# Attention and a mixture of experts in one kernel: queries and keys turned through DRAM, projections in pairs, inverse roots by log and exp

## The chip, the cores and the metric

The kernel runs on one core of a Trainium2 chip. The metric is the device time of one execution in microseconds (us), lower is better. The engines have a name each in the profile: PE is TensorE (matmuls; PEld its weight loads), DVE is VectorE, ACT is ScalarE, POOL is GpSimd, SP is SyncE, which here only issues DMAs.

## What is computed

The input x has 16 batches of 512 rows of 128 numbers, all in 32-bit floats. After a layer norm, two branches read the same normalised rows, and both are added to x:

```python
def _l2norm(t):
    n = jnp.sqrt(jnp.sum(t * t, axis=-1, keepdims=True))
    return t / jnp.maximum(n, EPS)
...
q, k, v = (proj(Wq), proj(Wk), proj(Wv))      # 16 heads of 8 numbers
q = _l2norm(q)
k = _l2norm(k)
sim = jnp.einsum('bhid,bhjd->bhij', q, k) * SCALE
sim = jnp.where(causal, mask_value, sim)
attn = jax.nn.softmax(sim, axis=-1)
o = jnp.einsum('bhij,bhjd->bhid', attn, v)
...
logits = jnp.einsum('bsh,eh->bse', x, Wr)     # 8 experts, the best 2 of each row
probs = jax.nn.softmax(logits, axis=-1)
top_v, top_i = jax.lax.top_k(probs, K)
for e in range(E):
    h = jax.nn.gelu(jnp.einsum('bsh,mh->bsm', x, W1[e]) + b1[e], approximate=False)
    y = jnp.einsum('bsm,hm->bsh', h, W2[e]) + b2[e]
    out = out + y * w_e[..., None]
...
x = x + attention(xn) + experts(xn)
```

## The kernel before

The kernel has three parts in time. First come the attention of batches 0 to 13 with the routing of all rows to experts beside it, then 71 expert blocks of 256 rows each, and last the attention of batches 14 and 15, beside which the experts' results are fetched and added.

A batch's attention is ten stages (`PER = 10`; `PAIR = 5` stages for two of the four groups of heads). Stage t of the whole program issues, in this order: the scores of stage t (`scores`, L665, into two of three PSUM buffers of the pool `ps_sim`, each of two banks) and their two exponentials on ScalarE (L675); one side step on TensorE in the first 21 stages (turning normalised rows, router logits); the causal masks of the stage before, on VectorE (L686) or GpSimd; the weighted sums of the stage two before (`LAG = 2`; `weigh`, L708, all into the one PSUM tile `av`), and after the last sums of a head group, in stages 1, 4, 6 and 9 of a batch, the transpose of `av` into `mid` on VectorE (L720); and then whatever `plan` holds for that stage (`due`). TensorE, VectorE, ScalarE and SyncE run their instructions in exactly the order in which these calls are written, so the numbers given to `at_stage` decide who stands behind whom. GpSimd keeps an order of its own through `on_pool` (L502), where the 128 indirect DMAs that send rows to the experts' slots are interleaved with squares and masks.

`prep(b)` puts the preparation of a batch into `plan`, at stages counted from its own first stage `t0`:

```python
times = (-18, -17, -14, -11) if b > 1 else (-11, -11, -10, -9)
...
    (-7, lambda: values(2)), (-7, sums), (-7, root_start), (-7, root_step),
    (-6, root_step), (-5, root_step), (-4, scale), (-3, turn_q), (-2, turn_k),
    (-2, lambda: alone(0)), (-1, lambda: alone(1)), (0, lambda: alone(2)),
    (b != B - 1, lambda: alone(3)),
```

`proj` projects 128 rows to q, k and v at once (L561) into the single PSUM buffer `misc`, which transposes, router logits and the output projection also use, and ScalarE copies the result to `qkv` (L564). GpSimd squares q and k (`squares`) and copies v into `vaug` (`values`). `sums` adds the squares by head on VectorE (L585), `root_start` takes the maximum with a tiny number (L600) and guesses the inverse root by integer arithmetic, and three calls of `root_step` refine it with three small VectorE instructions each (L211 to L213). `scale` (L608) multiplies. `turn_q` and `turn_k` turn the rows by four TensorE transposes each into `misc` (L619, L626) and copy the result on VectorE (L621, L628). `alone(r)` (L634) makes the keys' quarter r of `kT`, in which all but one head in four is zero. The first batch is prepared at the start of the program, with Sqrt on ScalarE and a reciprocal. `finish(b)` divides by the softmax's sums, turns the result and applies the output projection (`wout`, L752).

An expert block loads its rows and both weights (`fetch`, six buffers, five blocks ahead), turns the rows (L796), and does two matmuls (L817, L828) with a Gelu between (L820).

Of the kernel before, what the change touches and what calls it, by code (L numbers as in the profile page):

```python
# [10 lines left out]
F32 = mybir.dt.float32  # L11
# [6 lines left out]
HEADS = 16  # L18
# [6 lines left out]
def attention_moe_kernel(  # L25
# [45 lines left out]
    FIRST = B - 2  # L71
    AHEAD = (FIRST - 1) // 2
# [101 lines left out]
    def SIM(name):  # L174
# [4 lines left out]
        p1.tile([P, NC, HEADS, VW], F32, tag=f"vaug{n}", name=f"vaug{n}") for n in range(2)  # L179
# [34 lines left out]

    def guess(y, var):

        nc.vector.tensor_scalar(
            y.bitcast(I32), var.bitcast(I32), -0.5, float(0x5F3759DF), ALU.mult, ALU.add
        )
        nc.vector.tensor_single_scalar(var, var, -0.5, ALU.mult)  # L220

    def scales(b0, b1, root):
# [7 lines left out]
        def variance():  # L230
# [9 lines left out]
            if root:  # L240
                nc.scalar.activation(var, var, AF.Sqrt)

        def first():
            guess(rstd[:, cols], have["var"])
            newton(rstd[:, cols], have["var"], have["dif"], 1)

        def second():
            newton(rstd[:, cols], have["var"], have["dif"], 2)

        def shifts():  # L250
            if root:
                nc.vector.reciprocal(rstd[:, cols], have["var"])
            dif = have["dif"]
            nc.vector.tensor_add(dif, even, odd)
            nc.vector.scalar_tensor_tensor(
                shift[:, cols], dif, -0.5, rstd[:, cols], ALU.mult, ALU.mult
            )

        return [variance, shifts] if root else [variance, first, second, shifts]
# [14 lines left out]
    def turn_x(b, bank, copy):  # L274
# [3 lines left out]
        copy(xnT[b], bank)  # L278

# [271 lines left out]
    def prep(b):  # L551
# [3 lines left out]
        s["vaug"] = vaugs[b % 2]  # L555

        def proj(c, bank=misc):
            if not c:
                s["qkv"] = p2.tile([P, NC, NQKV], F32, tag="qkv", name=f"qkv{b}")
            pp = bank(f"proj{b}_{c}")  # L560
            nc.tensor.matmul(  # L561
                pp[:, :NQKV], xnT[b][:, ts(c, P)], wall, start=True, stop=True
            )
            nc.scalar.copy(s["qkv"][:, c], pp[:, :NQKV])  # L564

        heads = lambda t: t.rearrange("p c (h d) -> p c h d", d=DH)

# [5 lines left out]

        def values(c):
            on_pool(
                nc.gpsimd.tensor_copy,
                s["vaug"][:, c : c + 2, :, 0:DH],
                heads(s["qkv"][:, c : c + 2, 2 * D : 3 * D]),
            )
# [9 lines left out]
        def root_now(meanwhile):  # L589
# [3 lines left out]
            nc.scalar.activation(s["ss"], s["ss"], AF.Sqrt)  # L593
            meanwhile()
            nc.vector.reciprocal(s["rn"], s["ss"])

        def root_start():

            s["rn"] = sm.tile([P, n], F32, tag="rn", name=f"rn{b}", bufs=1)
            nc.vector.tensor_scalar_max(s["ss"], s["ss"], L2_EPS * L2_EPS)  # L600
            guess(s["rn"], s["ss"])

        def root_step():
            t = sm.tile([P, n], F32, tag="t", name=f"t{b}")
            newton(s["rn"], s["ss"], t, 1)

        def scale():
            nc.vector.tensor_mul(  # L608
                heads(s["qkn"]),
                heads(s["qkv"][:, :, : 2 * D]),  # L610
                s["rn"].rearrange("p (c h) -> p c h", c=NC).unsqueeze(3).to_broadcast(
                    [P, NC, 2 * HEADS, DH]
                ),
            )

        def turn_q():
            pt = misc(f"qt{b}")
            for c in range(NC):
                nc.tensor.transpose(pt[:, ts(c, P)], s["qkn"][:, c, :D], ident)  # L619
            s["qT"] = p2.tile([P, S], F32, tag="qT", name=f"qT{b}")  # L620
            nc.vector.tensor_copy(s["qT"], pt)  # L621

        def turn_k(bank=misc):
            pt = bank(f"kt{b}")
            for c in range(NC):
                nc.tensor.transpose(pt[:, ts(c, P)], s["qkn"][:, c, D:], ident)  # L626
            s["kr"] = p1.tile([P, S], F32, tag="turned", name=f"kr{b}")
# [532 lines left out]
```

## Time and profile before

| what | value |
|---|---|
| median of 3 runs | 779.11 us (777.05 to 779.11) |
| time of the profiled execution | 773.95 us |
| its span, first to last instruction | 772.2 us, mean granted TensorE clock 0.986 |
| start, up to the first scores | 0 to 27.3 us |
| attention of batches 0 to 13, with routing | 27.3 to 430.7 us |
| expert blocks | 430.7 to 707.0 us |
| attention of batches 14 and 15 | 707.0 to 772.2 us |

A row of the timeline gives start and duration in us, engine, line of the kernel, operation, output and inputs, shapes, how many instructions are merged in it, and in brackets how long the engine was idle before and what released it. TensorE's durations overlap a little, as its matmuls are pipelined; the distance from one start to the next is what an instruction costs there.

### The profile page before, as it was taken

What the parts mean: (1) busy time and instruction counts of PE and PEld (TensorE: products, weight loads), DVE (VectorE), ACT (ScalarE), POOL (GpSimd) and SP (SyncE); (2) the same over time, 40 slices, a digit from 0 to 9 for tenths busy, and PEclk for the clock granted to TensorE, in tenths of its full rate; (3) what the DMA queues carried; (4) which work ended last, traced back from release to release, by engine and by line L of the source; (5) the groups of instructions that cost most, each with busy time, mean ns of one, the idle gap of its engine ahead of it and who ended that gap; (6) DMA issues with size and microseconds to landing.
All of it is one profiled execution on the core that took longest, in us unless ns stands there. A gap on an engine that the chain in (4) does not pass through costs nothing.

```text
span 772.2 us, 17655 instructions
## 1 busy us (share of the span) xinstructions
PE 731.1 (95%) x6478; PEld 450.4 (58%) x6478; DVE 516.6 (67%) x1128; ACT 464.8 (60%) x703; POOL 485.9 (63%) x576
## 2 busy tenths in 40 slices
PE   6899999989999999999999899999999999998994
PEld 2344444334334444444444499989999999996441
DVE  6876678798987887887788445455554445442584
ACT  3767676567777778777878544433444444446771
POOL 4658444388898888888888255554555455556441
PEclk9999999999999999999999999999999999999996
DMA  9940000001101111110110698877777787850596
GB/s 264 326 149 2 1 2 1 1 20 32 33 29 37 37 34 33 36 37 29 38 37 32 194 280 229 229 223 210 235 222 226 222 233 224 233 167 6 187 283 183
DMA packets 91829, 96.48 MB, mean 125 GB/s; under 512 B 10956, under 2 KB 69455, under 8 KB 91744
## 3 DMA queue, kind: packets, MB, share of 16 engines
q1 hardware_dynamic: 82240, 78.01, 35.4%
q0 software_dynamic: 8640, 17.06, 6.5%
q8 instruction: 52, 0.85, 0.4%
q10 hardware_dynamic: 864, 0.28, 0.2%
q14 instruction: 33, 0.27, 0.1%
HBM read 64.34 MB, written 31.88 MB: 125 GB/s over the span
## 4 chain that ended last, share of the span: by engine, by line
PE 80%; DVE 14%; DMA 2%; ACT 1%; issue 1%; POOL 1%; DVEq 0%; POOLq 0%
PE sim L665 17%; PE av L708 17%; PE av L828 16%; PE ph L817 16%; PE proj L561 5%; DMA yt<-results 2%; DVE x L908 2%; PE xgt L796 2%; PE po L752 2%; DVE mid L720 1%; PE qt L619 1%; PE kt L626 1%; DVE st L206 1%; PE idle L959 1%; DVE kT L634 1%
## 5 line engine op out<-in xcount | busy, mean ns | idle before, releaser
L675 ACT ACTIVATE ex<-sim 128x1024 f32<-128x1024 f32 x320 | 310.0, 1022 | 105.4 <-PE sim L665 100.7
L502 POOL DMA_INDIRECT results<-y,to x142 | 139.0, 979 | 138.5 <-DVE y L836 111.8
L820 ACT ACTIVATE gT<-ph,bias 128x256 f32<-128x256 f32 x284 | 111.4, 475 | 158.4 <-PE ph L817 154.0
L665 PE MATMUL sim<-qT,kT 32*128 32x512 f32 (+3 forms) x2048 | 190.1, 463 | 0.7 <-ACT ex L675 0.7
L708 PE MATMUL av<-ex,vaug 128*12 128x512 f32 (+3 forms) x2048 | 171.5, 442 | 16.1 <-DVE mid L720 10.0
L502 POOL TENSOR_SCALAR_AFFINE_SELECT ex<-ex 128x512 f32<-128x512 f32 (+1 forms) x144 | 115.2, 808 | 84.3 <-ACT ex L675 82.6
L502 POOL DMA_INDIRECT slots<-rows,pos x128 | 140.7, 1099 | 28.8 <-issue 25.8
L665 PEld LDWEIGHTS sim<-qT,kT 32*128 32x128 f32 x2048 | 95.7, 185 | 77.8 <-issue 34.0
L828 PE MATMUL av<-xnT,gT 128*128 128x128 f32 x1136 | 138.7, 275 | 1.4 <-ACT gT L820 0.9
L817 PE MATMUL ph<-xgT,xnT 128*128 128x256 f32 x568 | 134.7, 380 | 1.5 <-DVE xgT L798 1.5
L828 PEld LDWEIGHTS av<-xnT,gT 128*128 128x128 f32 x1136 | 132.4, 192 | 2.6 <-issue 1.5
L708 PEld LDWEIGHTS av<-ex,vaug 128*12 128x12 f32 x2048 | 43.0, 92 | 129.3 <-issue 85.5
L817 PEld LDWEIGHTS ph<-xgT,xnT 128*128 128x128 f32 x568 | 102.5, 190 | 13.4 <-DVE xgT L798 1.9
L798 DVE COPY xgT<-xgt 128x256 f32<-128x256 f32 x71 | 30.1, 424 | 68.9 <-PE xgt L796 68.7
L833 DVE TENSOR_TENSOR y<-av,bb 128x256 f32<-128x256 f32 x71 | 30.1, 425 | 67.2 <-PE av L828 67.2
L720 DVE STREAM_TRANSPOSE mid<-av 128x512 f32<-128x512 f32 x64 | 45.5, 711 | 40.6 <-PE av L708 40.4
L561 PE MATMUL proj<-wall,xnT 128*128 128x384 f32 x128 | 58.3, 542 | 5.4 <-DVE xnT L278 2.9
L502 POOL TENSOR_TENSOR qkn<-qkv 128x256 f32<-128x256 f32 x64 | 54.9, 867 | 9.9 <-ACT qkv L564 9.5
L686 DVE TENSOR_TENSOR ex<-ex,causal 128x1024 f32<-128x1024 f32 x40 | 52.0, 1300 | 3.4 <-ACT ex L675 3.4
L634 DVE TENSOR_SCALAR kT<-kr,hmask 128x512 f32<-128x512 f32 x64 | 40.5, 635 | 0.6
L564 ACT COPY qkv<-proj 128x384 f32<-128x384 f32 x64 | 30.9, 482 | 14.1 <-PE proj L561 13.9
L561 PEld LDWEIGHTS proj<-wall,xnT 128*128 128x128 f32 x128 | 19.5, 190 | 32.6 <-issue 16.3
(144 smaller groups left out, 584.8 us busy)
## 6 DMA issues: line engine op xcount, KB each, us to landing
xnT<-in_w1T_dram SPq DMA_DIRECT2D x71, 256.0 KB, 3.5
xnT<-in_w2T_dram SPq DMA_DIRECT2D x71, 256.0 KB
slots<-fill SPq DMA_DIRECT2D x48, 198.0 KB, 5.1
xg<-slots SPq DMA_DIRECT2D x71, 132.0 KB
yt<-results SPq DMA_DIRECT2D x16, 512.0 KB, 5.1
bb<-in_b_dram SPq DMA_DIRECT2D x71, 64.0 KB
x<-in_x_dram SPq DMA_DIRECT2D x16, 256.0 KB, 4.7
out_dram<-x SPq DMA_DIRECT2D x16, 256.0 KB, 5.5
```

The lines of the kernel that those rows point to most:

```text
L502: ins = op(*args, **kw)
L561: nc.tensor.matmul(pp[:, :NQKV], xnT[b][:, ts(c, P)], wall, start=True, stop=True)
L564: nc.scalar.copy(s["qkv"][:, c], pp[:, :NQKV])
L634: nc.vector.tensor_scalar_mul(s["kT"][:, r], s["kr"], hmask[:, r : r + 1])
L665: nc.tensor.matmul(halves[g // 2][:, g % 2, col : col + (NC - j) * P], s["kT"][group, r, ts(j, P)], s["qT"][group, j * P :], start=True, s ...
L675: nc.scalar.activation(ex[:, 2 * h : 2 * h + 2], half, AF.Exp, scale=SCALE)
L686: nc.vector.tensor_mul(diag, diag, causal.unsqueeze(1).unsqueeze(1).to_broadcast([P, NG, many, P]),)
L708: nc.tensor.matmul(av[32 * g : 32 * g + VW, j * P :], s["vaug"][:, j, NG * g + r], s[m][:, g, col : col + (NC - j) * P], start=(j == 0), s ...
L720: nc.vector.transpose(s["mid"][:, r], av)
L817: nc.tensor.matmul(ph[:, m], s["w1"][:, ts(m, P)], s["xgT"], start=True, stop=True)
L820: nc.scalar.activation(s["gT"][:, m], ph[:, m], AF.Gelu, bias=bias1[:, i, m : m + 1])
L828: nc.tensor.matmul(py[:, c], s["gT"][:, m, ts(c, P)], s["w2"][:, m], start=(m == 0), stop=(m == NM - 1),)
```

## The change

For batches 3 and later, q and k no longer go through TensorE to change axes. `scale` writes the scaled rows ordered by blocks of 32 numbers, `carry` sends them to a DRAM buffer in four DMAs, each of which takes a quarter of the rows apart into runs of 128 numbers (512 bytes), and a fifth DMA brings them back with the 32-blocks where they belong. What is then left to do is a transpose of 32x32 blocks on VectorE, for q two stages and for k one stage ahead of the batch. All DMAs are issued by SyncE.

Two projections share one of the scores' PSUM buffers, with one copy of q and k for both and one of v, both on ScalarE, v directly into one of three `vaug` tiles. There is one `qkv` buffer in place of two, without v in it.

The inverse roots of the layer norm and of q and k are exp(-ln(v)/2) on ScalarE with one refining step on VectorE, except in the last batch, where the guess and three steps remain. One table with both functions is loaded at the start. Several steps get other stages: the sums and the root come earlier, the first `alone` later in the batches that are carried, and the finishing of a batch one or two stages later. Some of the routing steps move too.

```diff
+    CARRIED = 3
...
-        p1.tile([P, NC, HEADS, VW], F32, tag=f"vaug{n}", name=f"vaug{n}") for n in range(2)
+        p1.tile([P, NC, HEADS, VW], F32, tag=f"vaug{n}", name=f"vaug{n}") for n in range(3)
...
+    def inverse_root(y, var):
+
+        nc.scalar.activation(y, var, AF.Ln)
+        nc.scalar.activation(y, y, AF.Exp, scale=-0.5)
+
+    def refine(y, var, t, steps=1):
+        nc.vector.tensor_single_scalar(var, var, -0.5, ALU.mult)
+        newton(y, var, t, steps)
...
-            if root:
-                nc.scalar.activation(var, var, AF.Sqrt)
...
+            inverse_root(rstd[:, cols], var)
...
+    NF = D // TB
+
+    def berth(name):
+        return dram.tile([NF, TB, 2 * S], F32, tag="berth", name=name, bufs=2)
...
-        def proj(c, bank=misc):
+        def proj(c):
+
             if not c:
-                s["qkv"] = p2.tile([P, NC, NQKV], F32, tag="qkv", name=f"qkv{b}")
-            pp = bank(f"proj{b}_{c}")
-            nc.tensor.matmul(
-                pp[:, :NQKV], xnT[b][:, ts(c, P)], wall, start=True, stop=True
-            )
-            nc.scalar.copy(s["qkv"][:, c], pp[:, :NQKV])
+                s["qkv"] = p1.tile([P, NC, 2 * D], F32, tag="qkv", name=f"qkv{b}")
+            pp = s["pp"] = ps_sim.tile([P, 2, S], F32, tag="sim", name=f"proj{b}_{c}")
+            for k in range(2):
+                nc.tensor.matmul(
+                    pp[:, k, :NQKV], xnT[b][:, ts(c + k, P)], wall, start=True, stop=True
+                )
+                if not b:
+                    nc.scalar.copy(s["qkv"][:, c + k], pp[:, k, : 2 * D])
+            if b:
+                nc.scalar.copy(s["qkv"][:, c : c + 2], pp[:, :, : 2 * D])
+            return lambda: nc.scalar.copy(
+                s["vaug"][:, c : c + 2, :, 0:DH], heads(pp[:, :, 2 * D : NQKV])
+            )
...
+            (inverse_root if b < B - 1 else guess)(s["rn"], s["ss"])
...
+            refine(s["rn"], s["ss"], t, 1 if b < B - 1 else 3)
...
+            if b >= CARRIED:
+                to = s["qkn"].rearrange("p c w -> p (c w)").rearrange(
+                    "p (k c h d) -> p c k h d", c=NC, k=2 * NF, d=DH
+                )
...
+        def carry():
+
+            out_there = berth(f"bqk{b}")
+            to = out_there.rearrange("f i (k t w) -> t i k f w", k=2, t=P // TB)
+            by_block = s["qkn"].rearrange("p c w -> p (c w)").rearrange(
+                "p (k f w) -> p k f w", k=2, f=NF
+            )
+            for t in range(P // TB):
+                nc.sync.dma_start(to[t], by_block[ts(t, TB)])
+            s["z"] = p1.tile([P, 2, S], F32, tag="z", name=f"z{b}")
+            nc.sync.dma_start(
+                s["z"].rearrange("p k s -> p (k s)"),
+                out_there.rearrange("f i n -> (f i) n"),
+            )
+
+        def landed(k):
+            return s["z"][:, k].rearrange("p (t c w) -> p c t w", t=P // TB, c=NC)
...
         def turn_q():
+            s["qT"] = p2.tile([P, S], F32, tag="qT", name=f"qT{b}")
+            if "z" in s:
+                nc.vector.transpose(s["qT"], landed(0))
+                return
...
         def turn_k(bank=misc):
+            s["kr"] = p1.tile([P, S], F32, tag="turned", name=f"kr{b}")
+            if "z" in s:
+                nc.vector.transpose(s["kr"], landed(1))
+                return
...
-        times = (-18, -17, -14, -11) if b > 1 else (-11, -11, -10, -9)
...
-            (-11, lambda: squares(0)), (-11, lambda: squares(1)),
-            (-10 + (b == 1), lambda: squares(2)), (-9 + (b == 1), lambda: squares(3)),
-            (-8, lambda: values(0)),
-            (-7, lambda: values(2)), (-7, sums), (-7, root_start), (-7, root_step),
-            (-6, root_step), (-5, root_step), (-4, scale), (-3, turn_q), (-2, turn_k),
-            (-2, lambda: alone(0)), (-1, lambda: alone(1)), (0, lambda: alone(2)),
-            (b != B - 1, lambda: alone(3)),
...
+        if b >= CARRIED:
+            twos, squared = ((0, -14), (2, -12)), (-13, -13, -11, -10)
+            steps = [
+                (-9, sums), (-9, root), (-7, root_step), (-7, scale), (-7, carry),
+                (-2, turn_q), (-1, turn_k), (-1, lambda: alone(0)),
+            ]
+        else:
+            twos = ((0, -14), (2, -12)) if b > 1 else ((0, -11), (2, -10))
+            squared = (-13, -13, -11, -10) if b > 1 else (-11, -11, -9, -9)
+            steps = [
+                (-7, sums), (-7, root), (-5, root_step), (-4, scale), (-3, turn_q),
+                (-2, turn_k), (-2, lambda: alone(0)),
+            ]
+        for c, t in twos:
+            at_stage(t0 + t, lambda c=c: proj(c)())
+        for c, t in enumerate(squared):
+            at_stage(t0 + t, lambda c=c: squares(c))
+        steps += [(-1, lambda: alone(1)), (0, lambda: alone(2))]
+        for t, step in steps + [(b != B - 1, lambda: alone(3))]:
             at_stage(t0 + t, step)
...
-            at_stage(t0 - 1, lambda: product(0, NG))
-        for n, step in ((0, turn), (2, wout)):
-            at_stage(t0 + n, step)
+            at_stage(t0, lambda: product(0, NG))
+            for n, step in ((2, turn), (3, wout)):
+                at_stage(t0 + n, step)
...
+    nc.scalar.add_instruction(
+        mybir.InstLoadActFuncSet(name=nc.get_next_instruction_name(), act_func_set_id=6)
+    )
```

## The prediction

> **What bounds the kernel now.** I read the page's busy shares and slices first, then the chain that ended last, then one batch of the timeline engine by engine.
>
> ```profile
> PE 731.1 (95%) x6478; PEld 450.4 (58%) x6478; DVE 516.6 (67%) x1128; ACT 464.8 (60%) x703; POOL 485.9 (63%) x576
> PE   6899999989999999999999899999999999998994
> ...
> PE 80%; DVE 14%; DMA 2%; ACT 1%; issue 1%; POOL 1%; DVEq 0%; POOLq 0%
> ```
>
> TensorE is busy in every slice but the first and the last few, and the chain is 80% TensorE. So a TensorE instruction that goes away is worth its full time, and a new wait of TensorE costs its full time. From 234.0 us to 430 us the timeline repeats every 26.49 us (one batch, ten stages) with no TensorE gap over 0.3 us. Two places of that period carry this prediction. The first is the seam between two batches, TensorE's rows and then VectorE's:
>
> ```profile
> 322.52 0.66 PE L626 MATMUL kt<-ident,qkn 128*128 128x128 f32 x4
> 323.10 1.15 PE L665 MATMUL sim<-qT,kT 32*128 32x384 f32 x16
> 324.18 0.62 PE L708 MATMUL av<-ex,vaug 128*12 128x256 f32 x8
> 324.73 0.91 PE L561 MATMUL proj<-wall,xnT 128*128 128x384 f32 x2
> 325.57 1.14 PE L665 MATMUL sim<-qT,kT 32*128 32x512 f32 x8
> ```
> ```profile
> 323.21 0.69 DVE L628 COPY kr<-kt 128x512 f32<-128x512 f32 x1 [1.95 <-PE kt L626]
> 323.94 0.63 DVE L634 TENSOR_SCALAR kT<-kr,hmask 128x512 f32<-128x512 f32 x1
> 324.87 0.72 DVE L720 STREAM_TRANSPOSE mid<-av 128x512 f32<-128x512 f32 x1 [0.31 <-PE av L708]
> 325.51 0.45 DVE L634 TENSOR_SCALAR kT<-kr,hmask 128x512 f32<-128x512 f32 x1
> ```
>
> The new batch's first scores (325.57) read kT, whose first quarter was ready at 324.57, a microsecond early, because the keys were turned a stage before. The second place is two stages later (ScalarE, TensorE, VectorE):
>
> ```profile
> 302.81 3.94 ACT L675 ACTIVATE ex<-sim 128x1024 f32<-128x1024 f32 x4 [0.61 <-PE sim L665]
> ```
> ```profile
> 303.63 1.39 PE L665 MATMUL sim<-qT,kT 32*128 32x256 f32 x16
> 305.00 1.05 PE L708 MATMUL av<-ex,vaug 128*12 128x512 f32 x8
> ```
> ```profile
> 303.77 0.72 DVE L720 STREAM_TRANSPOSE mid<-av 128x512 f32<-128x512 f32 x1 [1.63 <-PE av L708]
> 304.41 0.83 DVE L634 TENSOR_SCALAR kT<-kr,hmask 128x512 f32<-128x512 f32 x1
> ...
> 308.10 1.18 DVE L585 TENSOR_REDUCE ss<-qkn 128x128 f32<-128x1024 f32 x1
> 309.31 0.86 DVE L600 TENSOR_SCALAR ss<-ss 128x128 f32<-128x128 f32 x1
> ```
>
> ScalarE does four exponentials without a pause here, right behind TensorE. TensorE has three score buffers and takes two per stage, so an exponential that is late by more than about a microsecond stops the next scores but one. Last, what a ScalarE instruction that waits for VectorE does to those behind it, from the start of the run:
>
> ```profile
> 19.50 0.40 DVE L592 TENSOR_SCALAR ss<-ss 128x128 f32<-128x128 f32 x1
> 19.93 0.31 ACT L593 ACTIVATE ss<-ss 128x128 f32<-128x128 f32 x1 [1.45 <-DVE ss L592]
> 20.14 0.57 ACT L278 COPY xnT<-xnt 128x512 f32<-128x512 f32 x1
> ```
>
> The copy's matmuls were over at 18.86; it ran only after the root, which waited 1.45 us for VectorE.
>
> **The change, part by part.**
>
> *Transposes of q and k removed* (batches 3 to 15). From 322.52 to 323.10 four of them take 0.58 us of TensorE, eight take 1.16: 13 x 1.16 = **-15.1 us**, all on the path. The two PSUM copies on VectorE (0.69 each) become two block transposes; the nearest row is `mid`, 0.72, so VectorE is as busy as before.
>
> *The trip through DRAM.* Each batch writes 512 KB as 1,024 runs of 512 bytes in four DMAs and reads 512 KB back in rows of 4 KB. The page gives 82,240 packets on SP's queue for 35.4% of 16 engines x 772 us: 53 ns each. 64 runs per engine come to 3.4 us; the row `yt`, also 512 KB, lands in 5.1. With SP's 0.33 to 0.45 us per issue: 1.6 + 3.5 + 0.4 + 5.1 = 10.6 us, estimated. The Trainium skill speaks against such a trip: "VectorE: DVE Perf Modes", The three transpose paths, calls a plain DMA that transposes by its access pattern 19 times slower than the hardware's DMA transpose, for which its table gives 1309 ns per 128x128 block of two bytes. By estimate that is 25 us for a block and 200 for a batch's eight, and the kernel would take over 2 ms. But the rule's condition is a large innermost stride; here innermost runs are contiguous and the 32x32 turning is VectorE's, so I take the row. What is there to hide it: let T be the end of stage 1's weighted sums (303.63 above). VectorE has the maximum done near T + 3.6 (wait B below), then a mask 1.2, reciprocal and product 1.2 to 1.7, four refining steps 1.1 to 2.4 and the scaling 1.2: rows ready near T + 9.3. It asks for q at the end of stage 8, after 17.2 us of TensorE's own rows and 3.0 of wait B, at T + 20.2; 2.7 us more would still cost nothing, as VectorE next waits for TensorE anyway. So zero, with some 3 us of cover. If that is gone, each further microsecond stops VectorE, and TensorE at the seam, 11 times. SP holds nothing else then; with batch 15 the weight fetches stand behind it, five blocks of 3.73 us ahead of their use: zero.
>
> *Wait A, at the seam.* In the changed program batches 3 to 13 turn the keys and mask the first quarter in the last stage before their own scores, behind `mid`, which waits for that stage's weighted sums; the projection that stood on TensorE there is gone. From the end of those sums: 0.14 until `mid` starts, 0.64 to the next instruction, 0.73 for the keys' transpose up to its reader (323.21 to 323.94), 0.63 for the mask, 0.1 to release: 2.24 us with TensorE idle, 1.9 to 2.5 by the shorter and longer rows of L634. I take 2.2: 11 x 2.2 = **+24.2**.
>
> *Wait B, the logarithm.* Root by Ln and Exp puts two ScalarE instructions behind stage 1's exponentials and ahead of stage 2's; Ln waits for VectorE. From T: 0.14 + 0.64 for `mid`, 0.75 for the last mask, 1.21 for the sums, 0.79 for the maximum (L600: mean 747 ns, extremes 0.23 and 1.5), so Ln starts at T + 3.6; the nearest row for it and for Exp is L593, 0.31 each, so the next exponential starts near 4.3 and its buffer is free at 5.4. TensorE wants it after scores (1.08), sums (0.98) and half of the next scores (0.54), at 2.6. Wait: 2.8, from 1.7 to 3.5 by the extremes of L600 and L634. In batches 3 to 14: 12 x 2.8 = **+33.6**, and 0.2 each for ScalarE catching up, **+2.4**. The two waits add, since T moves with A.
>
> *Early roots.* Batches 1 and 2 and the last twelve batches' scales also wait on ScalarE for a loaded VectorE, and in stages 6 and 16 the copy of a new batch waits for the scaling of the last, as there is one qkv buffer now. No row shows it; by the 1.45 above about 1 us each, **+5** (0 to 9). VectorE's own saving, seven small instructions or some 2.7 us a batch, lies beside TensorE: nothing. For batch 15 three refinements and the scaling stand in one place among the expert blocks, 4.3 us against 3.1 before, when a block took 2.4 us longer: **+1.3**.
>
> *Projections in pairs, in the scores' buffers.* Same TensorE work; values now copied by ScalarE (estimated 0.4 twice, for POOL's 0.47 twice), beside longer stages: nothing. Gone are TensorE's waits for the single misc bank (0.79, 0.79, 0.34, 0.56, 0.23, 0.72, 0.38, 0.58, 0.79 up to 151 us): **-5.2**; 1.06 before the first expert block: **-1.1**.
>
> *Waits that shrink as TensorE is later:* 0.29 at stage 2's scores, 11 times, **-3.2**; POOL's (2.20, 0.88, 0.60, 0.89, 0.57 from 166 to 231 us), most: **-4.0**.
>
> *Tables.* Sqrt goes, and with it the second table load, at 24.06 us. The row is 1.28 us with Exp right behind; "ScalarE: Activation LUTs", What ACT_TABLE_LOAD costs, counts 2.66 with its drain. Either way TensorE was held by projections in the misc bank there: **-0.5**, between nothing and 1.3.
>
> Sum: +66.5 - 29.1 = **+37.4**. Against the profiled execution of 774.0 that is 811.4; the median of the runs shown is 779.1, 5 us above it, and I put the sum on that: **816.5 us**.
>
> **Rivals.**
>
> 1. *Faster.* VectorE reaches the first mask and the maximum before TensorE needs them. Without A, B, their follow-up and half of the early waits: 66.5 - 60.2 - 2.5 = 3.8, less 29.1, 754 us. It decides where A and B together fall under some 2.0 us a batch instead of 5.0. For it: VectorE is 67% busy and the order of steps could spare one. Against: both waits start from TensorE's own last sums, which VectorE cannot have earlier. 0.11, with another 0.03 for within 0.3% (what a measurement of this kernel can tell from no change).
> 2. *The trip is late.* At 20 us instead of 10.6, VectorE's wait exceeds its cover by some 6: 11 x 6 = 66, 882 us. Against: DMA busy share 0.11 between 162 and 431 us. 0.05.
> 3. *Ln and Exp don't share a table,* two loads of 1.28 a batch: +33, 850 us. Against: three table loads stand in the changed program, four before. 0.01.
>
> The likeliest, A and B as worked out, has 0.80. Its ends: A 21 to 27, B 20 to 42, follow-up 0 to 7, early 0 to 9, removed waits half to all; not all at one end together, 786 to 838. I keep that as the range: it leaves out most of the faster case and the late trip.
>
> **What would show it.** A batch of near 30 us in place of 26.5; TensorE idle before first scores for VectorE's kT, about 2.2 us; ScalarE idle some 2.5 us before Ln, and TensorE waiting for an exponential one stage later. No `qt`, `kt` in batches 3 to 15, z in SBUF before VectorE asks. I am wrong if batches come out under 26.5 us, or if VectorE waits for a DMA at qT.

## The result, and the profile after

The changed kernel takes 835.93 us in the median of four runs (831.47 to 839.77), the kernel before 779.11 beside it: ratio 1.073, 95% interval 1.068 to 1.079, slower. The profiled execution took 831.47 us (span 829.7, mean granted TensorE clock 0.965; before 0.986), 57.5 us more span than before. The page has for TensorE's busy time, its slices, the granted clock and the chain that ended last:

```profile
PE 756.4 (91%) x6374; PEld 458.7 (55%) x6374; DVE 473.4 (57%) x1036; ACT 469.5 (57%) x737; POOL 459.8 (55%) x544
...
PE   6899999898979988988988979999999999999994
...
PEclk9999997999999999999989999999999999999996
...
PE 79%; DVE 12%; ACT 3%; issue 2%; DMA 1%; POOL 1%; ACTq 0%; POOLq 0%
```

TensorE has 104 instructions fewer and is busy 25 us longer, and its slices have nine eights and two sevens, where they had four eights before. The starts of rows place the 57.5 us (us; an output projection, `po`, ends each batch's work):

| from, to | before | after | more |
|---|---|---|---|
| start, first output projection | 77.4 | 82.2 | 4.8 |
| to the fourth | 97.3 | 98.9 | 1.6 |
| to the thirteenth (nine batches) | 242.6 | 290.9 | 48.3 |
| to the first expert block | 15.4 | 12.1 | -3.3 |
| first to last expert block | 265.5 | 272.4 | 6.9 |
| to the end | 74.1 | 73.2 | -0.9 |

Five of the nine batches take 30.8 to 31.0 us in place of 26.49, the other four 33.7 to 35.0. The seam between two batches, TensorE's rows and then VectorE's:

```profile
321.75 1.15 PE L700 MATMUL sim<-qT,kT 32*128 32x384 f32 x16
322.82 0.62 PE L743 MATMUL av<-ex,vaug 128*12 128x256 f32 x8
325.49 1.14 PE L700 MATMUL sim<-qT,kT 32*128 32x512 f32 x8 [2.04 <-DVE kT L662]
```
```profile
323.51 0.72 DVE L755 STREAM_TRANSPOSE mid<-av 128x512 f32<-128x512 f32 x1 [5.97 <-PE av L743]
324.15 0.67 DVE L651 STREAM_TRANSPOSE kr<-z 128x512 f32<-128x512 f32 x1
324.86 1.24 DVE L662 TENSOR_SCALAR kT<-kr,hmask 128x512 f32<-128x512 f32 x2
```

The first scores of the batch (325.49) now stand still for 2.04 us: `mid`, the keys' transpose and the first mask follow each other on VectorE behind TensorE's own last sums. Two stages later, ScalarE and then TensorE:

```profile
333.36 0.31 ACT L218 ACTIVATE rn<-ss 128x128 f32<-128x128 f32 x1 [2.21 <-DVE ss L600]
333.70 0.31 ACT L219 ACTIVATE rn<-rn 128x128 f32<-128x128 f32 x1
333.92 3.75 ACT L710 ACTIVATE ex<-sim 128x1024 f32<-128x1024 f32 x4
```
```profile
332.62 1.13 PE L700 MATMUL sim<-qT,kT 32*128 32x512 f32 x4
334.98 1.13 PE L700 MATMUL sim<-qT,kT 32*128 32x512 f32 x4 [1.23 <-ACT ex L710]
336.03 1.05 PE L743 MATMUL av<-ex,vaug 128*12 128x384 f32 x16
337.02 1.15 PE L700 MATMUL sim<-qT,kT 32*128 32x384 f32 x16
338.10 0.62 PE L743 MATMUL av<-ex,vaug 128*12 128x256 f32 x8
338.65 2.14 PE L700 MATMUL sim<-qT,kT 32*128 32x512 f32 x8
340.72 0.62 PE L743 MATMUL av<-ex,vaug 128*12 128x512 f32 x4
```

Ln waits 2.21 us for VectorE's maximum with the next exponentials behind it, and the scores that need their buffer take from 332.62 to 336.03, 3.41 us in place of 1.07. The bracket says 1.23 only. Two stages on (338.65 to 340.72) scores take 2.07 in place of 1.07, with no bracket at all. The single matmuls in these rows show why: before, four scores start together (at 312.44, and the next four at 312.97); here they start two at a time (338.65, 339.18, 339.66, 340.20), the four of one buffer first and then the four of the other, whose weight load waits for a semaphore. So TensorE is at work all the time, but on half as many scores at once, and distances between starts are the safer reading. The view of waits, over the whole span (total us, times, longest), TensorE and then ScalarE (before, the first of these waits did not occur and the second was 0.7 us in all):

```profile
PE sim L700 <- DVE kT L662: 22.6, 11, 3.0
PE sim L700 <- ACT ex L710: 16.5, 13, 2.9
```
```profile
ACT rn L218 <- DVE ss L600: 26.9, 14, 2.5
```

The trip through DRAM is not seen in the time: for the batch that begins at 325.49 its first DMA is issued at 308.09, its last packet lands at 316.40, and VectorE turns q at 316.84 without waiting. It is just in time, though; over the 13 batches VectorE waits twice for it, 0.6 us in all.

**The clock.** The trace has stretches of 3.41 us, or a multiple of it, in which the granted TensorE clock is half; they are called half-clock windows here. Below the trace is read in windows of 3.41 us laid on the instants at which the granted clock changes, with TensorE's busy time and count first and PEclk third from the end:

```profile
191.02:194.44 3.42, 2.83 (x28) 1.22 (x26) 0.35 (x1) 2.61 (x5) 3.00 (x3) 1.00 0.12 40
194.44:197.85 3.41, 1.68 (x16) 0.61 (x20) 3.38 (x5) 1.33 (x2) 3.21 (x5) 0.98 0.12 42
197.85:201.26 3.41, 3.41 (x32) 1.31 (x20) 0.88 (x2) 1.43 (x2) 2.93 (x4) 0.52 0.06 20
...
259.29:262.70 3.41, 2.56 (x27) 1.04 (x25) 0.79 (x2) 2.41 (x5) 3.06 (x5) 1.00 0.12 40
262.70:266.12 3.42, 2.23 (x24) 0.69 (x24) 3.30 (x5) 1.69 (x3) 2.93 (x4) 1.00 0.12 40
266.12:269.53 3.41, 3.41 (x56) 2.04 (x48) 0.37 (x1) 2.79 (x3) 2.74 (x4) 1.00 0.13 40
```

At 194.0 to 196.2 the seam's gap falls almost whole into one window (1.73 us of it), and the next window runs at half clock. At 262 the same gap is cut by a window's edge (0.85 and 1.18 us), and the clock stays. Before the last stretch of the span there are thirteen such half-clock windows in the changed kernel, and every one follows a window in which TensorE was idle for 1.1 us or more, or another half-clock window. The kernel before has two.

### The profile page after: what moved, and what is told of

Its sections match the earlier page's. It is cut to its first block, busy times and chain, and to the rows that moved or that the text cites. A ratio compares the mean times of both kernels' runs of the same rounds, so it can differ in the third digit from the quotient of the medians.

```text
span 829.7 us, 17476 instructions
## 1 busy us (share of the span) xinstructions
PE 756.4 (91%) x6374; PEld 458.7 (55%) x6374; DVE 473.4 (57%) x1036; ACT 469.5 (57%) x737; POOL 459.8 (55%) x544
## 4 chain that ended last, share of the span: by engine, by line
PE 79%; DVE 12%; ACT 3%; issue 2%; DMA 1%; POOL 1%; ACTq 0%; POOLq 0%
PE sim L700 20%; PE av L743 18%; PE av L865 15%; PE ph L854 15%; PE proj L572 5%; DVE x L945 2%; DVE mid L755 2%; PE po L787 2%; PE xgt L833 2%; DVE ss L593 2%; ACT ex L710 2%; DVE kT L662 2%; DMA yt<-results 1%; DVE st L207 1%; PE xnt L277 1%
## 5 line engine op out<-in xcount | busy, mean ns | idle before, releaser
L700 PE MATMUL sim<-qT,kT 32*128 32x512 f32 (+3 forms) x2048 | 226.8, 475 | 41.2 <-DVE kT L662 22.6
L700 PEld LDWEIGHTS sim<-qT,kT 32*128 32x128 f32 x2048 | 109.1, 191 | 153.3 <-ACT ex L710 81.3
L509 POOL TENSOR_SCALAR_AFFINE_SELECT ex<-ex 128x512 f32<-128x512 f32 (+1 forms) x142 | 118.3, 841 | 130.5 <-ACT ex L710 122.2
L743 PE MATMUL av<-ex,vaug 128*12 128x512 f32 (+3 forms) x2048 | 179.1, 459 | 8.7 <-DVE mid L755 6.6
L509 POOL DMA_INDIRECT slots<-rows,pos x128 | 135.0, 1055 | 28.0 <-issue 23.9
L854 PE MATMUL ph<-xgT,xnT 128*128 128x256 f32 x568 | 137.8, 386 | 5.9 <-issue 3.5
L509 POOL TENSOR_TENSOR qkn<-qkv 128x256 f32<-128x256 f32 x64 | 44.0, 697 | 42.3 <-issue 20.6
L572 PE MATMUL proj<-wall,xnT 128*128 128x384 f32 x128 | 49.7, 510 | 1.6 <-ACT qkv L576 0.9
L662 DVE TENSOR_SCALAR kT<-kr,hmask 128x512 f32<-128x512 f32 x64 | 36.9, 596 | 0.6
L873 DVE TENSOR_TENSOR y<-y,gate 128x256 f32<-128x256 f32 x71 | 30.2, 425 | 2.4
```

The lines of the kernel that those rows point to most:

```text
L509: ins = op(*args, **kw)
L572: nc.tensor.matmul(pp[:, k, :NQKV], xnT[b][:, ts(c + k, P)], wall, start=True, stop=True)
L662: nc.vector.tensor_scalar_mul(s["kT"][:, r], s["kr"], hmask[:, r : r + 1])
L700: nc.tensor.matmul(halves[g // 2][:, g % 2, col : col + (NC - j) * P], s["kT"][group, r, ts(j, P)], s["qT"][group, j * P :], start=True, s ...
L743: nc.tensor.matmul(av[32 * g : 32 * g + VW, j * P :], s["vaug"][:, j, NG * g + r], s[m][:, g, col : col + (NC - j) * P], start=(j == 0), s ...
L854: nc.tensor.matmul(ph[:, m], s["w1"][:, ts(m, P)], s["xgT"], start=True, stop=True)
```

## The experiments

Ratios are to the kernel before, timed beside each; five rounds each. A batch's length is the distance of output projections in the trace.

**1. The keys one stage earlier** (wait A alone).

```diff
-                (-2, turn_q), (-1, turn_k), (-1, lambda: alone(0)),
+                (-2, turn_q), (-2, turn_k), (-2, lambda: alone(0)),
```

> Only the keys' block transpose and the first mask (and so kT0) move from the last stage before their own scores to the stage before that; everything else is the changed kernel (835.9 us). Theory: wait A is real and additive: the 22.6 us that TensorE waits for kT in the trace go, and the half-clock windows that follow those waits go with them (each costs TensorE about 1.7 us of work, some 3 to 5 of them are at seams): 805 to 815 us, 1.03 to 1.05 of the kernel before, and no row of TensorE scores waiting for VectorE's kT above 0.3 us. Rival: VectorE is as late a stage earlier, because the turned data has not landed from DRAM or because VectorE is behind: then the wait only changes its name, within 8 us of 835.9.

813.03 us, ratio 1.038 (1.036 to 1.040), as the theory had it. The wait for kT falls from 22.6 to 0.3 us. In the execution with the trace (816.41 us, the slowest of five) the clock hardly changes (0.968 for 0.965): wait B is left, and half-clock windows still follow it, at 264, 295, 326 and 357 us. In the other four the clock is 0.976 to 0.980, above all four of the changed kernel (0.959 to 0.968), so clock is part of this gain too.

**2. Ln and Exp one stage later** (wait B alone).

```diff
-                (-9, sums), (-9, root), (-7, root_step), (-7, scale), (-7, carry),
+                (-9, sums), (-9, root), (-8, rooted), (-7, root_step), (-7, scale), (-7, carry),
```

(`root` keeps the maximum, `rooted` is the call of `inverse_root`.)

> Only Ln and Exp of the carried batches' roots move one stage later on ScalarE (behind stage 2's exponentials in place of ahead of them); sums and maximum stay where they are. Theory: wait B is the in-order ScalarE queue behind Ln: 12 x about 2.3 us of TensorE and some 1 us each of ScalarE catching up go, with the half-clock windows behind them: 785 to 805 us, 1.01 to 1.035 of the kernel before. Rival: the root only has a new place to hold up the exponentials, or VectorE, whose refinement follows a stage later, now waits for ScalarE and passes the wait on: within 10 us of 835.9.

816.52 us, ratio 1.042 (1.039 to 1.044): faster than the changed kernel, but less than expected. The waits for exponentials fall from 16.5 to 4.0 us and the clock rises to 0.978, while the weighted sums' wait for `mid` rises from 6.6 to 15.7 us, and an undisturbed batch is 30.0 us in place of 30.8. The wait for kT stays (24.1). So much of what wait B had cost came back as another wait, and a good part of the gain is clock: six half-clock windows before the last stretch in place of thirteen.

**3. Both moves.**

> Both moves together. Theory (A, B and the half-clock windows are the whole loss): granted clock back to 0.98 to 0.99, a batch back under 26.5 us, TensorE 15 us shorter than before by the transposes: 750 to 768 us, 0.96 to 0.985 of the kernel before. Rival 1: the trip through DRAM, no longer covered by wait B (some 3 us), is late: VectorE waits for z, up to 3 us a batch, 770 to 800 us. Rival 2: most of the loss is not in A and B but in the early roots and the DMA traffic: above 790 us.

805.88 us, ratio 1.030 (1.028 to 1.033): the second rival's time, but the rows below show another cause than the one it named. The clock is nearly back (0.983 in the trace, 0.974 to 0.983 in all five), the batch is 29.58 us. The two moves are worth 0.035 and 0.031 alone, taken from 1.073, and 0.043 together. The next batch's rows show what stands in their place, TensorE and then VectorE:

```profile
312.73 1.39 PE L704 MATMUL sim<-qT,kT 32*128 32x256 f32 x16
315.01 1.05 PE L747 MATMUL av<-ex,vaug 128*12 128x512 f32 x8 [0.89 <-POOL ex L509]
315.99 1.14 PE L704 MATMUL sim<-qT,kT 32*128 32x512 f32 x8
319.06 1.05 PE L747 MATMUL av<-ex,vaug 128*12 128x384 f32 x16 [1.93 <-DVE ex L725]
```
```profile
315.15 1.21 DVE L593 TENSOR_REDUCE ss<-qkn 128x128 f32<-128x1024 f32 x1
316.39 1.48 DVE L600 TENSOR_SCALAR ss<-ss 128x128 f32<-128x128 f32 x1
317.80 1.21 DVE L725 TENSOR_TENSOR ex<-ex,causal 128x1024 f32<-128x1024 f32 x1
```
```profile
316.68 1.11 POOL L509 TENSOR_SCALAR_AFFINE_SELECT ex<-ex 128x1024 f32<-128x1024 f32 x1
```

Sums and maximum, which the change put into stage 1, stand ahead of the mask of stage 1's exponentials (317.80), which the weighted sums at 319.06 want 1.93 us earlier. In the changed kernel wait B had covered that. The maximum (316.39) also takes 1.48 us here, and took 0.23 in the changed kernel (333.10 above): a mask of GpSimd runs beside it (last row). That is so in eight batches of this kernel, and in all the traces of this case this maximum takes over 0.7 us only where a GpSimd mask runs beside it for 0.7 us or more. So by the rows 1.25 of the 1.93 us go with what GpSimd does at that moment, and not with the order alone; no run separates the two. The trip, no longer covered by B, is nearly late (SyncE, then VectorE):

```profile
322.92 2.54 SPq L632 DMA_DIRECT2D bqk<-qkn  x4
328.42 0.33 SPq L634 DMA_DIRECT2D z<-bqk  x1
```
```profile
332.12 0.71 DVE L645 STREAM_TRANSPOSE qT<-z 128x512 f32<-128x512 f32 x1 [1.33 <-DMA z<-bqk]
```

It takes 9.2 us from its first issue (322.92) to VectorE's start; VectorE waits 6.3 us for it in all (1.5 at most), and TensorE waits 0.3 us for the keys. The first rival, as the cause of what is left, is out.

**4. Waits A and B filled with matmuls that nobody reads.**

```diff
+    def fill_wait(b, n):
+        for i in range(2):
+            nc.tensor.matmul(
+                misc(f"fill{b}_{n}_{i}")[:, :NQKV], ident, wall, start=True, stop=True
+            )
...
+        if n == 0 and CARRIED <= b < FIRST:
+            fill_wait(b, n)
...
+                if g == 2 and n == 3 and CARRIED - 1 <= b < FIRST:
+                    fill_wait(b, n)
```

> The changed kernel with two extra matmuls of constants (about 0.45 us each, their result is read by nobody) in front of the first scores of batches 3 to 13 and between the halves of stage 3's scores in batches 2 to 13, that is inside waits A and B. No other work is changed. Theory: the half-clock windows follow from idle TensorE time inside one 3.41 us window, so with the gaps cut from about 2.2 to 1.3 us most of the seven between 190 and 450 us vanish and the time falls by 7 to 13 us (823 to 829) though there is more work. Rival: they come from something else (power, DMA): they stay, and the time is 836 or up to 10 us longer by the extra matmuls.

All seven half-clock windows between 190 and 450 us are gone from the trace (clock 0.983; 0.981 to 0.989 in all six executions), and the edit only adds matmuls in and around TensorE's idle time: the windows follow from that idle time. The time, 832.01 us, is above the 823 to 829 expected; the ratio of 1.062 (1.059 to 1.065) lies 0.011 under the changed kernel's, some 9 us, with intervals that just do not touch. The matmuls were not free: an undisturbed batch is 32.0 us in place of 30.8.

**5. The same kernel as in 3 without the trip**, TensorE turning q and k.

```diff
-                (-9, sums), (-9, root), (-8, rooted), (-7, root_step), (-7, scale), (-7, carry),
+                (-9, sums), (-9, root), (-8, rooted), (-7, root_step), (-7, scale),
...
-            if b >= CARRIED:
+            if False:
```

(The second edit leaves out the block order of `scale`.)

> The kernel with both moves (keys a stage earlier, root a stage later; 805.9 us, 1.030 of the kernel before), but queries and keys of all batches are turned by TensorE and a VectorE copy at the same stages, with no trip through DRAM. Theory: the trip is hidden (in the kernel with both moves it takes 9.2 us and VectorE waits 6.3 us for it in all) and the transposes are pure TensorE time on the path, 13 x 1.16 = 15.1 us: 818 to 823 us, 1.045 to 1.053, a batch of 30.7 us in place of 29.58. Rival: the batch is set by VectorE's waits behind the maximum, so TensorE's transposes fill time that was idle anyway or the trip's DMAs cost something elsewhere: 800 to 810 us.

859.62 us, ratio 1.103 (1.100 to 1.106), 0.072 more than with the trip: neither case. The view of waits, GpSimd:

```profile
POOL qkn L509 <- PE kt L659: 102.6, 14, 8.8
```

There is one `qkn` tile. The keys' transpose on TensorE reads it until stage 8, and the next batch's squares, which the change put into stages 7 and 9, wait for it on GpSimd, with causal masks behind them in order; TensorE's sums then wait 40.1 us for masks. The trip reads `qkn` out at stage 3. That it frees this tile early is what lets the squares, and with them the sums and the root, move forward with one such tile.

**6. The same with `qkn` in two buffers.**

```diff
-                s["qkn"] = p1.tile([P, NC, 2 * D], F32, tag="qkn", name=f"qkn{b}")
+                s["qkn"] = p2.tile([P, NC, 2 * D], F32, tag="qkn", name=f"qkn{b}")
```

> The kernel no_trip (859.6 us; both moves, queries and keys turned by TensorE) with one more edit: qkn in two buffers. Theory: no_trip was slow because the keys' transpose reads qkn until stage 8 while GpSimd's squares of the next batch, moved to stages 7 and 9, want to write it: GpSimd waits 102.6 us there in the trace, in order, with the masks behind. With two buffers that wait goes and only the transposes' own TensorE time is left over the kernel with both moves (805.9): 815 to 825 us, 1.043 to 1.055 of the kernel before. Rival: the transposes meet a VectorE or PSUM wait of their own (10.9 us of kt waiting for the copy of qt in the trace): 830 to 860.

805.65 us, ratio 1.041 (1.039 to 1.042). The 102.6 us are gone, so that cause is shown. Against the kernel with the trip it is 0.010 slower by the ratios (8 us), and 0.5 us by the two spans (804.5 and 804.0; batches of 29.53 and 29.58). So going without the trip cost 0.5 to 8 us there, and not 15.1. But this is a balance, and it does not isolate the transposes: the keys' transposes wait 10.6 us in all for the copy of `qt` (both turns stand in one stage here), a wait for `mid` of 0.79 us is new in a batch, and on the other side the wait of 0.89 us is gone and the one of 1.93 shrinks to 0.36. The last is for the most part the maximum, which takes 0.23 us in this kernel, with no mask of GpSimd beside it, and 1.48 in the other.

**7. The pairs without the trip and without Ln** for q and k: `guess` and three refinements at the stages of before.

```diff
-    CARRIED = 3
+    CARRIED = B
...
-            (inverse_root if b < B - 1 else guess)(s["rn"], s["ss"])
+            (guess if b else inverse_root)(s["rn"], s["ss"])
...
-                (-7, sums), (-7, root), (-5, root_step), (-4, scale), (-3, turn_q),
+                (-7, sums), (-7, root), (-7, root_step), (-6, more_steps),
+                (-5, more_steps), (-4, scale), (-3, turn_q),
```

> The changed kernel without the trip and with the q and k roots of batches 1 to 15 by the guess and three refinements on VectorE at the stages of the kernel before (qkv in two buffers). What is left of the change: projections in pairs in the score buffers with the values copied by ScalarE, products and output projections a stage later, the early roots of the norms by Ln and Exp. Theory: the pairs alone cost about 0.67 us at the first scores and 0.19 at the ninth of each batch, because ScalarE's two copies (0.97 us) hold up an exponential and a pair holds a score buffer: a batch of 27.3 us in place of 26.49, +8 to +10 in all, less the 5 us of misc-bank waits that go, with the early roots +5: 785 to 795, 1.005 to 1.02 of the kernel before. Rival (the prediction's term): the pairs cost nothing and save 5 to 13 us: 768 to 780.

(`qkv` has two buffers again.) 831.58 us, ratio 1.066 (1.063 to 1.070): a miss, because this kernel too keeps early squares and one `qkn` (81.7 us on GpSimd behind `kt`). It does not isolate the pairs; the next one comes closer.

**8. The same with the squares at the stages of before.**

```diff
-            squared = (-13, -13, -11, -10) if b > 1 else (-11, -11, -9, -9)
+            squared = (-11, -11, -10, -9) if b > 1 else (-11, -11, -9, -9)
```

> The kernel pairs_alone (831.6 us) with the squares of batches 2 to 15 at the stages of the kernel before (one stage 9, one stage 9, stage 0, stage 1 in place of 7, 7, 9, 0), after the keys' transposes have read qkn. Theory: its 33.6 us of weighted sums waiting for GpSimd's masks come from squares waiting for qkn (81.7 us of GpSimd time behind kt): they go, and what is left is the pairs' own price of about 0.9 us a batch by ScalarE's copies and the score buffer: 785 to 800 us, 1.005 to 1.025. Rival (the prediction's): the pairs cost nothing: 768 to 780. Rival 2: the wait has another cause: above 815.

779.38 us, ratio 1.007 (1.006 to 1.009), with a batch of 27.21 us. The microseconds alone lie in the rival's range, but the kernel before took 773.50 beside it; ratio and batch are the theory's. So what is left of the change costs 0.7 us a batch. Its rows at the seam:

```profile
353.28 1.15 PE L705 MATMUL sim<-qT,kT 32*128 32x384 f32 x16
354.36 0.62 PE L748 MATMUL av<-ex,vaug 128*12 128x256 f32 x8
354.91 1.82 PE L705 MATMUL sim<-qT,kT 32*128 32x512 f32 x8
356.66 1.48 PE L748 MATMUL av<-ex,vaug 128*12 128x512 f32 x16
```

The scores at 354.91 take 1.75 us in place of 1.07, and those of stage 5 1.57.

**9. What costs the 0.7 us.** In the kernel of 3 with the root a stage earlier (see 10), projections again one at a time in the misc bank:

```diff
+        if b > CARRIED:
+            squared = (-15, -13, -12, -11)
+            for c, t in enumerate((-16, -14, -13, -12)):
+                at_stage(t0 + t, lambda c=c: single(c))
+            twos = ()
```

> The kernel root_a_stage_earlier with the projections of batches 4 to 15 one at a time in the misc bank (stages 4, 6, 7 and 8; two ScalarE copies each) in place of pairs in the score buffers. Theory: a pair holds a score buffer until ScalarE has made both its copies, and the scores behind it wait some 1 us a batch in all (0.67 at the first scores, 0.3 at the eighth, more at the sixth): a batch of 27.6 to 28.0 us in place of 28.77, 777 to 783 us, 0.995 to 1.004 of the kernel before. Rival: what holds the scores is ScalarE's own time (four copies of 256 and four of 128 columns now, about 0.6 us a batch more), not the buffer: 789 to 800.

798.02 us, ratio 1.020 (1.015 to 1.024), against 1.011 with pairs: the pair's buffer is not the reason, the scores at the seam still take 1.75 us (330.67 to 332.42 there). In the timeline ScalarE has finished all earlier work there and waits 0.59 us for TensorE's scores; it is TensorE that comes back too early for the next free buffer. Between the scores of stage 9 and those of stage 0 it has 1.63 us of work and ScalarE 1.94 us of exponentials. The same holds for stage 4, and the kernel before had a projection (0.84) in the one and the output projection (1.09) in the other. So, on top of 8, these two places filled as before:

```diff
-            twos = ((0, -14), (2, -12)) if b > 1 else ((0, -11), (2, -10))
+            twos = ((0, -14), (2, -11)) if b > 1 else ((0, -11), (2, -10))
...
-            at_stage(t0, lambda: product(0, NG))
-            for n, step in ((2, turn), (3, wout)):
+            at_stage(t0 - 1, lambda: product(0, NG))
+            for n, step in ((0, turn), (2, wout)):
```

> The kernel pairs_late_squares (1.0072 of the kernel before, a batch of 27.21 us) with two pieces of TensorE work put back where the kernel before had them: the second projection pair of batches 2 to 15 in stage 9, and product, turn and output projection a stage earlier, so that the output projection stands in stage 4. Theory: stages 4 and 9 are the short ones of TensorE (scores 1.08 and weighted sums 0.55, 1.63 us, against 1.94 us of exponentials on ScalarE), so the scores behind them (stage 5: 1.58 us, stage 0: 1.75 us, in place of 1.07) wait for an exponential unless other TensorE work stands there; the kernel before had 1.09 and 0.84 us of it there. Put back, both waits go: a batch of 26.0 to 26.2 us, 27.21 less 0.67 and 0.51, and 765 to 773 us for 778, 0.986 to 0.998 of the kernel before. Rival: the pair's two copies (0.97 us) on ScalarE, wherever they stand, hold up the next exponentials: 27.0 to 27.5 us a batch, 1.003 to 1.012.

772.25 us, ratio 0.999 (0.997 to 1.001). The same place again:

```profile
349.57 0.62 PE L748 MATMUL av<-ex,vaug 128*12 128x256 f32 x8
350.12 1.56 PE L572 MATMUL proj<-wall,xnT 128*128 128x384 f32 x4
351.61 1.24 PE L705 MATMUL sim<-qT,kT 32*128 32x512 f32 x8
352.79 1.48 PE L748 MATMUL av<-ex,vaug 128*12 128x512 f32 x16
```

With the pair in between, the scores take 1.18 us, and those of stage 5 1.35. So the two short stages were the cause of most of it (0.56 of 0.72 us); they were filled together, and not one by one. The batch is 26.65 us, half a microsecond above the theory; small waits for a mask (0.16) and for `mid` (0.21) are new. No version tried beats the kernel before; this one equals it.

**10. What was left in the kernel of 3.** Sums and maximum ahead of the mask's turn, in stage 0, and all that follows one stage earlier:

```diff
-            twos, squared = ((0, -14), (2, -12)), (-13, -13, -11, -10)
+            twos, squared = ((0, -14), (2, -12)), (-13, -13, -11, -11)
...
-                (-9, sums), (-9, root), (-8, rooted), (-7, root_step), (-7, scale), (-7, carry),
+                (-10, sums), (-10, root), (-9, rooted), (-8, root_step), (-8, scale), (-8, carry),
```

> The kernel with both moves, and now sums and maximum in the first stage of a batch (ahead of the last weighted sums of the batch before), Ln and Exp behind the second stage's exponentials, refinement, scaling and the trip one stage earlier too; the last square moves a stage earlier on GpSimd for it. Theory: what is left of the loss in the kernel with both moves is the mask of the second stage's exponentials behind sums and maximum on VectorE (1.95 us a batch): it goes, 11 x 1.95 = 21 us, 780 to 788 us, 0.995 to 1.007 of the kernel before. Rival: sums now wait for GpSimd's last square or hold up the seam (mid, kT), and a wait of 1 to 2 us a batch comes back under another name: 795 to 815.

789.32 us, ratio 1.011 (1.007 to 1.014), a little above the theory: the mask's 1.93 us are gone from the rows and a batch is 28.77 us, but weighted sums wait 18.1 us for `mid` over the span, up from 11.4. With the scaling and the trip two stages later:

```diff
-                (-10, sums), (-10, root), (-9, rooted), (-8, root_step), (-8, scale), (-8, carry),
+                (-10, sums), (-10, root), (-9, rooted), (-8, root_step), (-6, scale), (-6, carry),
```

> The kernel root_a_stage_earlier (789.3 us, 1.011 of the kernel before, a batch of 28.77 us) with the scaling and the trip moved two stages later, behind the transpose of the third weighted sums; the refinement stays. Theory: the 0.74 us that weighted sums wait for mid there go, and the trip (9.2 us), now asked for some 3 us earlier than it lands, is hidden all the same, because VectorE has 4 us idle before the seam: 779 to 785 us, 0.998 to 1.006. Rival: the late trip passes on to the masks on VectorE or to kT: 792 to 810, with VectorE waits for z of 2 us and more.

792.30 us, ratio 1.012 (1.008 to 1.016), no difference from the run before that these intervals show, and the rival's time and its waits of VectorE rather than the theory's. VectorE waits 19.5 us for z, up to 3.0 at a time, the wait for `mid` halves (9.3), the batch is 28.07 us, and the expert blocks and single longer batches take it back. For kT TensorE still waits 0.3 us in all, although z is up to 3 us late for VectorE. What sets the rest of the batch was not followed further.

## Why the prediction was right and wrong

Slower was right, and by the mechanism named as the likeliest: both waits stand in the trace where the prediction put them. 835.93 lies just inside the upper end of the range (838), 19 us above the number, and that it lies inside is partly luck: the ends were worked out without the clock, which turned out to be the largest term left out. Step by step:

- **Trip hidden, 0.** Right in effect, and near in size: 9.2 us against 10.6 estimated. The rule of the Trainium skill, "VectorE: DVE Perf Modes", The three transpose paths, would by the prediction's estimate have made it 200 us; the trip with contiguous runs of 512 bytes and the 32x32 turning left to VectorE is far from that. No run has a trip with a large innermost stride, so the rule itself is not tested. The cover was smaller than the 3 us claimed as long as VectorE is looked at: z landed 8.3 us after the first issue in the rows above and q was turned 0.4 us later. TensorE had more: in scale_later VectorE waits up to 3.0 us and TensorE does not wait longer for kT. The prediction's sign of being wrong, VectorE waiting for a DMA at qT, did show, but with 0.6 us in all. What the step missed is that the trip frees `qkn`.
- **Wait A, +24.2.** 22.6 in the waits, and 1 shows that undoing it removes it.
- **Wait B, +33.6.** The mechanism is right; the size was 3.41 - 1.07 = 2.3 a batch, not 2.8. The maximum took 0.23 us after the sums there (333.10 in the trace) and not the 0.79 assumed; in the kernel before a GpSimd mask runs beside it in most batches, here in none of these. TensorE also asked 0.5 us later than assumed (3.1 after T), and lost as much by doing the scores two at a time.
- **ScalarE catching up, 0.2 a batch.** Mis-sized: the scores of stage 5 lose 1.0. And its cause was incomplete: about half is the short stage 4 from which the output projection was moved (8 shows 0.5 there with neither Ln nor trip). A prediction that moves a step must also ask what the place it leaves was covering.
- **Transposes, -15.1, "all on the path".** Within a batch the arithmetic holds: 2.05 + 2.34 + 1.0 + 0.4 (smaller delays) - 1.16 - 0.38 = 4.25 of the 4.31 us by which 30.80 exceeds 26.49. The -0.38 is the pairs' own saving, two of 1.49 for four of 0.84, which the prediction put at nothing. But when the large waits are gone, the kernel with the transposes is only 0.5 to 8 us slower than the one without (6), so their length is no longer a measure of what they cost.
- **Left out: the clock.** Eleven more half-clock windows, each costing up to half of 3.41 us, are at most 18.8 us. In the two batches at 34.1 and 33.9 us, against 30.8 undisturbed, it is 6.4 us for four windows, 1.6 each. By that estimate eleven windows are some 18 us, most of the gap of 20.1 us between the sum (+37.4) and the traces (+57.5); the rest is what the other misses, of both signs, leave over. This is the step that fell short: the waits were counted at their own length, as if idle time left no trace in the work after it.
- **First expert block, -1.1.** Wrong sign: block 0 took 7.34 us in place of 3.12. Wait A has a second form there: keys, masks and then the block's own copy queue on VectorE (484.2 to 487.9), TensorE stands for 3.49 us, and the block's eight matmuls of `ph` then run at half clock (3.58 us for 1.99).
- **Batch 15 among the experts, +1.3.** Right for the wait: TensorE's wait for `xgT` is 1.93 us in place of 0.67, 1.26 more. The block takes 7.36 for 4.66 us, 2.7 more, and a half-clock window follows that wait (573.2 us). That a block had taken 2.4 us longer before is misread; it took 4.66 us for the usual 3.73.
- **Early roots, +5.** The start lost 4.8, but the last kernel of 9, which has the same early roots of the norms, loses 1.8, so by that comparison those are about a third of it.
- **Rivals.** "Faster" wanted A and B gone; with both moved the kernel is still 1.030, so that rival had missed the mask behind them and the short stages. "The trip is late" is out, by the 0.6 us. Tables: Ln and Exp run back to back in the rows above; no load stands between them.

## What to carry to other kernels

Before moving a step, list what its old place was hiding, which tile its reads keep busy, and which queue it now heads: here the output projection was covering an exponential, the keys' transpose held a tile, and a root held the exponentials. When engines are this close to each other, taking one wait away shows the next, so waits do not add and should be undone together before a gain is promised. And a gap on TensorE can cost more than its length, since the clock may halve after it.

## What was unexpected in the hardware

A TensorE gap of about 2 us was enough to halve the granted clock for the next 3.41 us, if it lay within one window of a grid of that width; cut by an edge, it cost nothing more. Seven of seven such windows between 190 and 450 us vanished when the gaps were filled with matmuls that nobody reads. The Trainium skill, "TensorE: Matmul & The Clock Gate", Part 1, has the free-running window of 3413 ns, which agrees, and in its table of the two states the clock falls after at least one idle window; here windows with as little as 1.1 us of idle time did it, others of the same kernel with 1.3 to 1.8 did not, and one of the two in the kernel before (at 129.5 us) follows a window whose rows show no gap at all. So the busy time of a window does not decide alone, and what does was not found.

Two more readings are easy to miss. Scores that wait for one of their two buffers can leave no idle time at all: they run two at a time in place of four, and 1.07 us become 2.07. And the same maximum of 128x128 numbers on VectorE took 0.23 us alone and 1.48 with a mask of GpSimd beside it for 1.11 us.
